# A graph message-passing kernel: order of the set-up, keys of two groups spread by TensorE, another order at the end, and 358 selections for 355

## The chip, the cores and the metric

The kernel runs on one core of a Trainium2 chip. The metric is the device time of one execution in microseconds (us), less is better. The engines are TensorE (PE, matrix products; its weight loads are shown as PEld), VectorE (DVE), ScalarE (ACT), GpSimd (POOL) and SyncE (SP). SP, ACT and POOL have queues from which DMAs are issued; each engine takes its instructions in the order of the program.

## The reference

```python
# N = 6250 nodes, E = 200000 edges sorted by dst, F = H = 64, M = 9, D = 32; AVG_DEG = 16
w    = silu(edge_attr_32 @ W1 + b1) @ W2 + b2                 # E x 9
msg  = einsum('ef,em,fmg->eg', x[src], edge_attr_9 * w, W_tp) # E x 64
agg  = segment_sum(msg, dst, N) / sqrt(AVG_DEG)
emb  = silu(node_vec[:, None] @ Wn1 + bn1) @ Wn2 + bn2
gamma, beta = split(emb, 2)
out  = layernorm(x + agg * (1 + gamma) + beta)
```

Everything is float32.

## The kernel before, in words

**Groups.** The edges lie in 1563 tiles of 128 (`NT`), taken in 98 groups (`NBLK`) of 16 tiles (`KB`), the last one of 11. Since edges are sorted by destination, the 128 edges of a tile reach only a window of 8 nodes (`W`), and a group reaches 128 window columns.

**Rows of x.** A tile needs the 128 rows x[src], one to a partition, in `hs[g]`. They come in three ways. Most tiles are gathered by an indirect DMA on POOL (L91), one instruction to a tile, 6 groups ahead (`AHEAD`), with 7 buffers. In every sixth group (`SPG`: 7, 13, ..., 97) the first tile comes by 128 DMAs of one row each from SP's queue (`load_rows`, L106). And the last 3 or 4 tiles of a group are *picked* on TensorE: x stands in SBUF as seven slices (`xs`), each number split in two parts whose sum it is; `pick(g, t)` multiplies a one-hot matrix (`hot_k`) with both parts of the seven slices, 14 matmuls into one PSUM tile `px` (L475), and DVE takes the wanted seventh of each result (`xm`, L484) and adds up (L486). `picked(g)` is the number of picked tiles of a group; in all there are 355 picked tiles, 1192 gathered ones and 16 that come by rows.

**Keys.** `hot_k` (DVE, L460) compares a key with a counter. The key of an edge must stand on all partitions, with edges along the free axis. Set-up computes the keys of all 392 picked columns with nine steps on DVE (L205 to L217), transposes them on TensorE in four pieces, stores them as float16 in DRAM (`kd`, L224), and `load_keys` reads those of two groups back, broadcast over the partitions (`kr`, L391). `keys(g)` copies a group's into PSUM on ACT (`pk`, L454).

**A group's other work.** `hidden(g)`: first layer on TensorE (L403) and silu on ACT (L411). `second(g)`: second layer (L420), bias on ACT (`p2s`, L423). `weights(g)`: two transposes (L430) and products on DVE that make `a`, 72 columns a tile (L442). `windows(g)`: for each tile one product of `hs` and `a` into `pz` (L504), which ACT copies to `zt` in four strided pieces for 8 tiles (L514). `project(q)`, for two groups: ten-fold product with W_tp (L543; L538 for the single last group), a transpose and the split in two parts `r`, and one-hot matrices `c` (L528). `place(q)`: puts the window columns to the nodes (`ps`, L559). `bring`: transposes back (L576) and calls `finish`, the gate, the residual and the layer norm for two blocks of 128 nodes (L670 to L683; the square root on ACT, L680), whose last line stores to `out`.

**Order.** There is no scheduler: all engines run the program's order. The loop over blocks `i` writes it out by hand: gather of group i+6; loads; rows by SP; `keys(i+2)`; `pick(i+1, 0)` with the node work of older groups among its matmuls; `hots`; `hidden(i+2)`; `second(i+1)`; `windows(i)`; `project` in odd blocks; `pick(i+1, 1)` with `weights(i+1)` and the transpose of `project` among its matmuls; the other picks of group i+1. The last two groups' `windows` come at the ends of their blocks.

**Set-up.** `setup` issues the loads, builds constants on POOL and DVE, gathers the first six groups, and splits x into `xs`: for each of seven slices ACT copies it, reordered, into PSUM (L292) and casts it to the first part (L293), and DVE subtracts for the second (L294). Among the slices stand the first keys and one-hot matrices, and `pick(0, 0)` follows the last slice. `base` spreads the first destination of each tile over the partitions with a product by ones (`p_b`, L242) and subtracts it from `dst` (`rel`, L243).

Of the kernel before, what the change touches and what calls it, by code (L numbers as in the profile page):

```python
# [7 lines left out]
F32 = mybir.dt.float32  # L8
# [41 lines left out]
def picked(g):  # L50

    return Q - (3 * g % 8 < 3)
# [7 lines left out]
def gnn_resnorm_kernel(ctx: ExitStack, tc: tile.TileContext, x, src, dst, dst_row, ea, sh, cn,  # L60
# [18 lines left out]
    with ExitStack() as fast:  # L79
# [54 lines left out]
        def setup(temp):  # L134
# [3 lines left out]
            nc.sync.dma_start(src_i[:, 0:AHEAD * KB], src[:, 0:AHEAD * KB])  # L138
            for q in range(4):
                nc.sync.dma_start(w1bd[q * D:(q + 1) * D, (q % 2) * H:(q % 2 + 1) * H], w1)  # L140
            nc.sync.dma_start(src_i[:, AHEAD * KB:], src[:, AHEAD * KB:])
            xb_r = xb.rearrange("p j f -> p (j f)")
            row_i = xb_r[0:1, 0:NBLK * KB].bitcast(I32)
            nc.scalar.dma_start(row_i, dst[0:1, :])
# [4 lines left out]
            for s in range(2):  # L149
                nc.scalar.dma_start(b1c[s * H:(s + 1) * H, :], b1.unsqueeze(1))  # L150

            xk = gam.rearrange("p (h l) f -> p h (l f)", h=J)
            x_v = x.rearrange("(p h l) f -> p h (l f)", h=J, l=J)
            for h0, h1 in ((0, 2), (2, 4), (4, 7)):
                nc.scalar.dma_start(xk[:, h0:h1, :], x_v[:, h0:h1, :])
            load(0)
            for s in range(2):
                nc.sync.dma_start(w2p[s * H:(s + 1) * H, s * M:(s + 1) * M], w2)
            nc.sync.dma_start(dst_i, dst)
# [18 lines left out]
            row_f = xb_r[0:1, NBLK * KB:2 * NBLK * KB]  # L178
            nc.scalar.copy(row_f, row_i)
            first_t = temp.tile([NBLK, KB], F32)  # L180
            nc.scalar.copy(first_t, first_i)
# [5 lines left out]
            nc.vector.tensor_add(ident2, ident[:, 0:F], ident[:, F:P])  # L187
            zero = temp.tile([P, 1], F32)
            nc.vector.memset(zero, 0.0)
            for k in range(2):  # L190
                nc.vector.memset(ht[k][H:H + 1], 1.0)
            nc.vector.memset(wtc2[F:P, 4], 0.0)
            ones1 = temp.tile([1, P], F32)
            nc.vector.memset(ones1, 1.0)
            nc.vector.memset(eps, EPS)
            nc.vector.tensor_copy(nk, nk_i)
            nc.vector.tensor_copy(wi, n_i[:, 0:W])
            nc.vector.tensor_copy(li, n_i[:, 0:J])


            zt_r = zt.rearrange("p a c k w -> p (a c k w)")
            s_f, kp, kh, rest, t0, t1 = [zt_r[:, k * C:(k + 1) * C] for k in range(6)]
            ti = [t.bitcast(I32) for t in (t0, t1)]
            s_f = s_f.rearrange("p (g k) -> p g k", k=Q)
            nc.vector.tensor_copy(s_f[:, 0:NBLK - 1, :],  # L205
                                  src_i.rearrange("p (g k) -> p g k", k=KB)[:, 0:NBLK - 1, KB - Q:])
            nc.vector.tensor_copy(s_f[:, NBLK - 1, :], src_i[:, NT - Q:NT])
            s_f = s_f.rearrange("p g k -> p (g k)")
            nc.vector.tensor_scalar(ti[0], s_f, 2675.0, None, op0=ALU.mult)
            nc.vector.tensor_scalar(ti[0], ti[0], 17, None, op0=ALU.logical_shift_right)  # L210
            nc.vector.tensor_copy(kp, ti[0])
            nc.vector.scalar_tensor_tensor(rest, kp, -float(J * J), s_f, op0=ALU.mult, op1=ALU.add)
            nc.vector.tensor_scalar(ti[1], rest, 37.0, None, op0=ALU.mult)
            nc.vector.tensor_scalar(ti[1], ti[1], 8, None, op0=ALU.logical_shift_right)
            nc.vector.tensor_scalar(kh, ti[1], float(P), None, op0=ALU.mult)
            kf = s_f
            nc.vector.tensor_add(kf, kp, kh)  # L217
            for c0 in range(0, C, P):
                n = min(P, C - c0)
                p_kt = psum.tile([P, P], F32, tag=("s", "r")[c0 // P % 2], name=f"p_kt{c0}")  # L220
                nc.tensor.transpose(p_kt[0:n], kf[:, c0:c0 + n], ident)
                kt = t1[:, c0 // 2:c0 // 2 + P // 2].bitcast(F16)
                nc.scalar.copy(kt[0:n], p_kt[0:n])
                nc.sync.dma_start(kd[c0:c0 + n, :], kt[0:n])  # L224
            nc.vector.scalar_tensor_tensor(jl, kh, -float(J) / P, rest, op0=ALU.mult, op1=ALU.add)
            hidden(0, act=False)
            load_keys(0)
            load_keys(LB)
            for c in range(KB // 4):
                for s in range(2):  # L230
                    q = c * D + s * M
                    nc.sync.dma_start(b2c[q:q + M, :], b2.unsqueeze(1))


            rel_v = rel.rearrange("p (a b c) -> p a b c", a=2, b=2)
            dst_v = dst_i.rearrange("p (a b c) -> p a b c", a=2, b=2)
            row_v = row_f.rearrange("p (a b c) -> p a b c", a=2, b=2)

            def base(a_):
                p_b = psum.tile([P, 2, KB * P // 4], F32, tag="p1", name=f"p_b{a_}")  # L240
                for b_ in range(2):
                    nc.tensor.matmul(p_b[:, b_, 0:NBLK * KB // 4], ones1, row_v[:, a_, b_, :], start=True, stop=True)  # L242
                nc.vector.tensor_sub(rel_v[:, a_], dst_v[:, a_], p_b[:, :, 0:NBLK * KB // 4])  # L243


# [8 lines left out]
            nc.vector.tensor_copy(pw, pw_i)  # L254

            def ids():
                p_nid = psum.tile([P, NBLK], F32, tag="s", name="p_nid")
                nc.tensor.matmul(p_nid, sel, first_f, start=True, stop=True)
                nc.vector.scalar_tensor_tensor(nid, p_nid, pw, lo, op0=ALU.add, op1=ALU.subtract)

            def between(h):

                if h == 0:
                    p_f = psum.tile([KB, NBLK], F32, tag="s", name="p_f")
                    nc.tensor.matmul(p_f, first_t, ident[0:NBLK, 0:NBLK], start=True, stop=True)
                    nc.scalar.copy(first_f, p_f)
                elif h == 1:
                    keys(0)
                    hots(0, 0, Q)
                elif h == 3:  # L270
                    p_cn = psum.tile([P, NJ], F32, tag="s", name="p_cn")
                    nc.tensor.matmul(p_cn, cn_j, ident[0:NJ, 0:NJ], start=True, stop=True)
                    cn_s = temp.tile([P, NJ], F32)
                    nc.scalar.copy(cn_s, p_cn)
                    nc.sync.dma_start(cn_d, cn_s)
                    nc.sync.dma_start(wn1c, wn1.rearrange("o h -> h o"))
                    nc.sync.dma_start(bn1c, bn1.unsqueeze(1))
                    gate_load(0)
# [10 lines left out]
            for h in range(J):  # L289
# [5 lines left out]
                if h == 1:  # L295
                    hidden_act(0)
# [13 lines left out]
            for f in weights(0):  # L310
                f()
# [547 lines left out]
```

## Time and profile before

| | us |
|---|---|
| timed runs: median of 3 (lowest, highest) | 2508.16 (2504.98, 2527.9) |
| profiled execution, own time | 1521.78 |
| profiled execution, span from first to last instruction | 1519.9 |
| PE busy | 1438.0 |
| POOL busy | 1129.3 |
| DVE busy | 1135.4 |
| ACT busy | 526.1 |

The mean granted TensorE clock of the profiled execution is 0.983. Its own time is 986 us under the median of the timed runs. The profile is one execution; busy time is the time in which an engine has an instruction in work, the idle time before an instruction is put down to what released it, and "issue" stands where the profile shows nothing that was waited for. Lines written L91 are those of the kernel before.

### The profile page before, as it was taken

To read this page: it belongs to the slowest core of one execution; us is meant where nothing else is said; L and a number is where in the kernel's file an instruction comes from. 1 tells how busy PE (TensorE), PEld (TensorE's weight loads), DVE (VectorE), ACT (ScalarE), POOL (GpSimd) and SP (SyncE) were. 2 spreads that over 40 slices of the span, in tenths; PEclk is the share of its full clock that TensorE was granted. 3 is DMA by queue.
4 is the path that set the end of the run, shared out by engine and by line. 5 is a ranking of instruction groups with operands and counts; after the bars stand their busy time and mean duration, and the time that the engine had idled before them with its cause. 6 is when DMAs were issued, how large, how long until landed. Compare 5 with 4: busy or idle time off the path is not lost.

```text
span 1519.9 us, 34363 instructions
## 1 busy us (share of the span) xinstructions
PE 1438.0 (95%) x10810; PEld 1192.7 (78%) x10810; DVE 1135.4 (75%) x1987; ACT 526.1 (35%) x1335; POOL 1129.3 (74%) x1201
## 2 busy tenths in 40 slices
PE   4998999999999999999999999989998998999995
PEld 2787888888888788888888888878777887878784
DVE  5686777877877878777777877768677777687773
ACT  4223342433423333332423424424233333333331
POOL 7777777777777777777777777777777777777772
PEclk9999999999999999999999999999999999999997
DMA  6422232222222222222322222222222222222210
GB/s 171 95 56 63 54 76 53 64 59 70 65 56 72 58 63 71 60 63 54 74 59 55 72 52 63 71 54 61 53 72 53 59 55 71 52 55 59 73 29 15
DMA packets 90939, 96.16 MB, mean 63 GB/s; under 512 B 37161, under 2 KB 51451, under 8 KB 90748
## 3 DMA queue, kind: packets, MB, share of 16 engines
q0 software_dynamic: 38144, 39.14, 13.4%
q1 hardware_dynamic: 51842, 53.09, 12.1%
q8 instruction: 88, 1.44, 0.4%
q10 hardware_dynamic: 762, 1.64, 0.3%
q14 instruction: 103, 0.84, 0.2%
HBM read 92.04 MB, written 1.73 MB: 62 GB/s over the span
## 4 chain that ended last, share of the span: by engine, by line
PE 57%; POOL 18%; issue 9%; SPq 5%; DMA 5%; DVE 4%; ACT 2%; DVEq 0%; POOLq 0%; ACTq 0%
PE px L475 41%; POOL hs L91 18%; PE pz L504 5%; DMA hs<-in_x_dram,src_i 4%; PE p L403 3%; SPq L106 3%; PE pt L543 3%; PE p L420 2%; SPq L101 2%; PE p L430 1%; PE ps L559 1%; PE ps L589 0%; ACT st L411 0%; DVE hot_k L460 0%; DVE xm L484 0%
## 5 line engine op out<-in xcount | busy, mean ns | idle before, releaser
L91 POOL DMA_INDIRECT hs<-in_x_dram,src_i x1192 | 1128.0, 946 | 364.3 <-issue 330.7
L475 PE MATMUL px<-xs,hot_k 128*128 128x448 f32 x4970 | 1090.6, 372 | 9.4 <-DVE xs L294 8.8
L475 PEld LDWEIGHTS px<-xs,hot_k 128*128 128x128 f32 x4970 | 896.8, 189 | 93.9 <-issue 10.9
L484 DVE SCALAR_TENSOR_TENSOR xm<-li,jl,px 128x448 f32<-128x448 f32 x355 | 240.3, 677 | 203.6 <-PE px L475 202.0
L460 DVE TENSOR_TENSOR hot_k<-pk,nk 128x896 fp32r<-128x896 f32 x355 | 370.6, 1082 | 3.1 <-ACT pk L454 3.1
L411 ACT ACTIVATE st<-p,b1c 128x1024 f32<-128x1024 f32 x98 | 109.5, 1118 | 405.4 <-PE p L403 405.1
L486 DVE TENSOR_REDUCE hs<-xm 128x64 f32<-128x448 f32 x355 | 220.1, 620 | 12.2
L514 ACT COPY zt<-pz 64x160 f32<-64x160 f32 (+2 forms) x784 | 213.5, 272 | 40.6 <-PE pz L504 28.0
L504 PEld LDWEIGHTS pz<-a,hs 128*64 128x64 f32 x3126 | 110.2, 142 | 68.1 <-issue 61.2
L504 PE MATMUL pz<-a,hs 128*64 128x72 f32 x3126 | 124.6, 234 | 27.0 <-DMA hs<-in_x_dram,src_i 11.5
L442 DVE TENSOR_TENSOR a<-oh,p 128x1152 f32<-128x1152 f32 x98 | 132.7, 1354 | 3.3
L436 DVE TENSOR_TENSOR p<-p,sh 128x72 f32<-128x72 f32 x196 | 47.0, 240 | 100.9 <-ACT rt L546 45.2
L403 PE MATMUL p<-ea,w1bd 64*128 64x512 f32 x392 | 113.3, 655 | 0.0
L565 ACT COPY carry<-ps 128x128 f32<-128x128 f32 x48 | 12.8, 266 | 273.4 <-PE ps L559 273.4
L420 PEld LDWEIGHTS p<-st,w2p 128*32 128x32 f32 x784 | 15.8, 108 | 83.2 <-issue 39.0
L420 PE MATMUL p<-st,w2p 128*32 128x256 f32 x784 | 63.5, 396 | 7.8 <-DVE xb L356 7.8
L680 ACT ACTIVATE var<-var,eps 128x2 f32<-128x2 f32 (+1 forms) x25 | 7.4, 295 | 179.2 <-DVE var L679 179.2
L543 PE MATMUL pt<-zt,wtc 128*64 128x128 f32 x960 | 64.3, 281 | 2.6 <-ACT zt L514 1.7
L543 PEld LDWEIGHTS pt<-zt,wtc 128*64 128x64 f32 x960 | 55.0, 142 | 3.8 <-ACT zt L514 1.9
L454 ACT CAST pk<-kr 128x384 f32<-128x384 f16 (+1 forms) x98 | 53.8, 549 | 2.2 <-DMA kr<-kd 2.2
L430 PE MATMUL p<-ident,p2s 128*128 128x128 f32 x196 | 53.3, 273 | 0.0
L403 PEld LDWEIGHTS p<-ea,w1bd 64*128 64x128 f32 x392 | 30.0, 187 | 28.7 <-issue 28.0
(122 smaller groups left out, 529.0 us busy)
## 6 DMA issues: line engine op xcount, KB each, us to landing
hs<-in_x_dram SPq DMA_DIRECT2D x2048, 0.2 KB
ea<-in_ea_dram SPq DMA_DIRECT2D x49, 512.0 KB
hs<-in_x_dram,src_i POOLq DMA_INDIRECT x1192
kr<-kd SPq DMA_DIRECT2D x49, 256.0 KB
sh<-in_sh_dram SPq DMA_DIRECT2D x49, 144.0 KB
cb<-cn_d SPq DMA_DIRECT2D x12, 128.0 KB
out_dram<-o SPq DMA_DIRECT2D x24, 64.0 KB
gam<-in_x_dram ACTq DMA_DIRECT2D x2, 448.0 KB
```

The costliest lines, as they stand in the source:

```text
L91: hs_dma[g] = [nc.gpsimd.indirect_dma_start(out=hs[g][:, t - g * KB, :], out_offset=None, in_=x, in_offset=bass.IndirectOffsetOnAxis(ap=sr ...
L403: nc.tensor.matmul(p1[:, i, :], w1bd[i * 64:(i + 1) * 64, :], e[i * 64:(i + 1) * 64, :], start=True, stop=True)
L411: nc.scalar.activation(st[g], p1_t.pop(g), AF.Silu, bias=b1c)
L420: nc.tensor.matmul(p2[g][c * D:(c + 1) * D, 0, :].rearrange("p (i e) -> p i e", i=2), w2p, s[:, :, c * P:(c + 1) * P], start=True, stop=True)
L442: nc.vector.tensor_mul(a[g], oh_t.pop(g)[:, :, None, :].to_broadcast([P, KB, M, W]), sw.unsqueeze(3).to_broadcast([P, KB, M, W]))
L460: nc.vector.tensor_tensor(hot_k[g, t], pk_t[g][:, t, None, :].to_broadcast([P, J, P]), nk.unsqueeze(2).to_broadcast([P, J, P]), op=ALU.is_ ...
L475: nc.tensor.matmul(px.rearrange("p f l -> p (f l)"), hot_k[g, t][:, h, :], xs[i][:, h].rearrange("p f l -> p (f l)"), start=(h == 0 and i ...
L484: nc.vector.scalar_tensor_tensor(xm, li[:, None, :].to_broadcast([P, F, J]), jl[:, c:c + 1], px, op0=ALU.is_equal, op1=ALU.mult)
L486: nc.vector.tensor_reduce(hs[g][:, tiles(g) - q + t, :], xm, AX.X, ALU.add)
L504: mm = nc.tensor.matmul(pz[v * F:(v + 1) * F, k // 2].rearrange("p m w -> p (m w)"), hsg[:, k0 + k, :], ag[:, k0 + k].rearrange("p m w -> ...
L514: nc.scalar.copy(z[h * F:(h + 1) * F, 0:5 - h, k0 + v:k0 + n:2, :].rearrange("p m k w -> p k m w"), pz[v * F:(v + 1) * F, 0:(n + 1 - v) // ...
L543: nc.tensor.matmul(pt[h * F:(h + 1) * F, 0, 0:P], wtc2[:, c, :], z[h][:, c], start=(c == 0), stop=(c == 4))
```

## The change

It has five parts.

1. **Set-up order.** The pieces of x go to the head of ACT's queue, in four DMAs for three. On SP's queue come the first sources, the first weights, the edge features of group 0 apart from those of group 1 (`load(0, split=True)`), and the first 32 columns of `dst` with their first destinations broadcast by DMA (`row_i`, for the product by ones of `base`). All else is loaded after group 0's work in the program.
2. **Splitting x.** The copy of each slice into PSUM is dropped; DVE subtracts from SBUF.
3. **Keys of groups 0 and 1.** `keys_of(0, LB)` works out 8 columns only; `keys_first` scales the identity by a key column on DVE and multiplies by a matrix of ones on TensorE, so that the key of edge e stands in column e on all partitions. The other 384 columns take the old way (`keys_rest`), after group 0's picks.
4. **The end.** `windows(96)` moves to its usual place. The picks of group 97 have `project(48)` and `place(48)` among them. `windows(97)` takes its second half of tiles, the picked ones, first, writes to two PSUM tiles, and half of its copies are DVE's. Stores of results are issued by SP at the start of the next block, in a list `stores`.
5. **358 picks.** Three picked tiles are 34 groups' (every third, and the last) in place of 37 groups'; three gathers fewer.

```diff
 def picked(g):
-    return Q - (3 * g % 8 < 3)
+    return Q - (g % 3 == 0 or g == NBLK - 1)
@@ setup
             nc.sync.dma_start(src_i[:, 0:AHEAD * KB], src[:, 0:AHEAD * KB])
+            xk = gam.rearrange("p (h l) f -> p h (l f)", h=J)
+            x_v = x.rearrange("(p h l) f -> p h (l f)", h=J, l=J)
+            for h0, h1 in ((0, 1), (1, 2), (2, 4), (4, 7)):
+                nc.scalar.dma_start(xk[:, h0:h1, :], x_v[:, h0:h1, :])
             for q in range(4):
                 nc.sync.dma_start(w1bd[q * D:(q + 1) * D, (q % 2) * H:(q % 2 + 1) * H], w1)
+            for s in range(2):
+                nc.scalar.dma_start(b1c[s * H:(s + 1) * H, :], b1.unsqueeze(1))
+            row_i = xb.rearrange("p j f -> p (j f)")[:, 0:NBLK * KB].bitcast(I32)
+            load(0, split=True)
+            nc.sync.dma_start(dst_i[:, 0:2 * KB], dst[:, 0:2 * KB])
+            nc.sync.dma_start(row_i[:, 0:2 * KB], rows(dst[0, 0:2 * KB], P))
             nc.sync.dma_start(src_i[:, AHEAD * KB:], src[:, AHEAD * KB:])
...
+            def keys_first(g, kf, tag):
+                pk_t[g] = psum.tile([P, Q, P], F32, tag=tag, name=f"pk{g}")
+                for t in range(picked(g)):
+                    c = (g + 1) * Q - picked(g) + t
+                    d0 = NBLK * KB + c * P
+                    dg = xb.rearrange("p j f -> p (j f)")[:, d0:d0 + P]
+                    nc.vector.tensor_scalar(dg, ident, kf[:, c:c + 1], None, op0=ALU.mult)
+                    nc.tensor.matmul(pk_t[g][:, t, :], ones, dg, start=True, stop=True)
+            def keys_rest(kf):
+                for c0 in range(LB * Q, C, P):
+                    n = min(P, C - c0)
+                    p_kt = psum.tile([P, P], F32, tag="r", name=f"p_kt{c0}")
+                    nc.tensor.transpose(p_kt[0:n], kf[:, c0 - LB * Q:c0 - LB * Q + n], ident)
+                    kt = zt_r[:, 6 * C + c0 // 2:6 * C + c0 // 2 + P // 2].bitcast(F16)
+                    nc.scalar.copy(kt[0:n], p_kt[0:n])
+                    nc.sync.dma_start(kd[c0:c0 + n, :], kt[0:n])
+            def split(h):
+                xh = gam[:, h * J:(h + 1) * J, :].rearrange("p l f -> p f l")
+                nc.scalar.copy(xs[0][:, h], xh)
+                nc.vector.tensor_sub(xs[1][:, h], xh, xs[0][:, h].bitcast(F32))
+            kf = keys_of(0, LB)
+            keys_first(0, kf, "r")
+            hots(0, 0, 1)
+            for h in range(J):
+                split(h)
+            pick(0, 0)
+            hots(0, 1, Q)
+            keys_first(1, kf, "s")
+            hots(1, 0, 1)
+            nc.vector.tensor_copy(wi, n_i[:, 0:W])
+            nc.vector.tensor_sub(rel[:, 0:2 * KB], dst_i[:, 0:2 * KB], row_i[:, 0:2 * KB])
+            near(0)
+            pick(0, 1)
+            hots(1, 1, Q)
+            hidden(0)
+            second(0)
+            pick(0, 2, [[lambda: None, lambda: None], weights(0)])
+            hidden(1)
+            nc.sync.dma_start(dst_i[:, 2 * KB:], dst[:, 2 * KB:])
+            nc.sync.dma_start(row_i[:, 2 * KB:], rows(dst[0, 2 * KB:], P))
+            load(LB)
+            keys_rest(keys_of(LB, NBLK))
+            load_keys(LB)
...
-                xp = psum.tile([P, F, J], F32, tag="px" if h in (2, 3) else "pz", name=f"x{h}", bufs=2)
-                nc.scalar.copy(xp, xh)
-                nc.scalar.copy(xs[0][:, h], xh)
-                nc.vector.tensor_sub(xs[1][:, h], xp, xs[0][:, h].bitcast(F32))
...
@@ windows
-            for k0 in range(0, nk, ZT):
+            end = g == NBLK - 1
+            for k0 in reversed(range(0, nk, ZT)) if end else range(0, nk, ZT):
...
-                        nc.scalar.copy(
+                        (nc.vector.tensor_copy if end and v else nc.scalar.copy)(
@@ blocks
+                while stores:
+                    stores.pop(0)()
...
-                if i < NBLK - 2:
+                if i < NBLK - 1:
                     windows(i)
-                turn = project(i // 2) if i % 2 == 1 else []
+                turn = project(i // 2) if i % 2 == 1 and i < NBLK - 1 else []
...
+                if i == NBLK - 2:
+                    sums(i + 1)
+                    turn = project(i // 2)
+                    ps = psum.tile([P, 2 * P], F32, tag="s", name="ps_l")
+                    pick(i + 1, 2, [turn])
+                    more = place(i // 2, ps)
+                    if picked(i + 1) < Q:
+                        for f in more:
+                            f()
+                        more = []
+                    pick(i + 1, 3, [more])
+                    continue
...
+            for f in bring(NJ - 3, NJ - 1, psum.tile([P, FB, F], F32, tag="s", name="py_l")):
+                f()
+            windows(NBLK - 1)
             project(NBLK // 2)
```

## The prediction

> **What bounds the kernel now.** First the page's busy shares, then the costliest groups, then the stretches of the span, the waits, and the timelines of start and end.
>
> ```profile
> PE 1438.0 (95%) x10810; PEld 1192.7 (78%) x10810; DVE 1135.4 (75%) x1987; ACT 526.1 (35%) x1335; POOL 1129.3 (74%) x1201
> L91 POOL DMA_INDIRECT hs<-in_x_dram,src_i x1192 | 1128.0, 946 | 364.3 <-issue 330.7
> L475 PE MATMUL px<-xs,hot_k 128*128 128x448 f32 x4970 | 1090.6, 372 | 9.4 <-DVE xs L294 8.8
> ```
>
> By busy time TensorE (PE) is the bound and POOL has a quarter to spare. That is the wrong reading: nearly all of POOL's idle time stands before gathers and is put down to "issue", nothing that it waits for. The timeline of POOL gives the real pace:
>
> ```profile
> 2.92 1.11 POOL L91 DMA_INDIRECT hs<-in_x_dram,src_i  x1 [0.97 <-DMA src_i<-in_src_dram]
> ...
> 1493.22 0.94 POOL L91 DMA_INDIRECT hs<-in_x_dram,src_i  x1 [0.30 <-issue]
> ```
>
> From the first start to the last are 1191 intervals in 1490.3 us: 1.2513 us each, with no stop between. POOL gathers from 2.9 us to 1494.2 us of a span of 1519.9. The stretches say where PE meets it:
>
> ```profile
> 600.00:800.00 200.00, 197.56 (x1533) 164.58 (x1532) 156.40 (x279) 71.62 (x185) 151.45 (x160) 1.00 0.27 63
> 1000.00:1200.00 200.00, 188.89 (x1394) 157.99 (x1389) 143.39 (x236) 64.43 (x168) 151.21 (x160) 0.98 0.26 62
> ```
>
> PE (first busy figure) is full until about 980 us and then loses 11 us in 200; POOL (fifth) is the same in both. In the waits of PE, its idle time before windows (L504) is a wait for gathered rows:
>
> ```profile
> PE pz L504 <- DMA hs<-in_x_dram,src_i: 11.5, 8, 4.4
> PE pz L504 <- issue: 10.8, 6, 4.8
> PE pz L504 <- DMA out_dram<-o: 2.5, 1, 2.5
> ```
>
> I read all three as that, since they begin where the last gather of the group ended only 2 to 3 us before: 24.8 us that PE has in hand. So the order is: group 0's windows at 55.75 us stand 36 us behind their gathers (the thirteenth gather, counted off on POOL, ended at 19.4), PE takes 14.7 us a group and POOL 15.2, the lead of POOL is eaten by about group 62, and from there POOL sets the pace. The last of it is in the timeline of PE:
>
> ```profile
> 1472.36 1.22 PE L504 MATMUL pz<-a,hs 128*64 128x72 f32 x32 [0.41 <-DMA hs<-in_x_dram,src_i]
> ...
> 1485.71 8.08 PE L475 MATMUL px<-xs,hot_k 128*128 128x448 f32 x38
> 1493.72 1.22 PE L504 MATMUL pz<-a,hs 128*64 128x72 f32 x32
> ...
> 1502.01 1.67 PE L504 MATMUL pz<-a,hs 128*64 128x72 f32 x22
> 1506.35 2.40 PE L538 MATMUL pt<-wtc,zt 128*128 128x64 f32 x10 [2.67 <-ACT zt L514]
> ```
>
> **What the Trainium skill says.** "Perfetto Trace Analysis", section GPSIMD Engine Instruction, calls a GpSimd span unreliable and asks for start-to-start spacing; the trace agrees: 1.2513 us against a printed 0.946. The same page, section DMA Instruction — SWDGE (GPSIMD), says that the end shown is that of the last descriptor and not of the data; here windows 95 begin at 1472.36, 1.9 us after the last gather of their group ended at 1470.5. "FP8 and Floating Point Precision", section TensorE Precision Notes, gives true FP32 four passes; no row here has a 128x128 FP32 product by a ones matrix, so I use the row of the key transposes below.
>
> **The change part by part.**
>
> *358 picks for 355.* Three gathers fewer: 3 x 1.2513 = 3.75 us off POOL. On PE three picks more: 28 pick matmuls took 6.74 us in the chain of waits (0.241 each), so 3 x 14 x 0.241 = 10.1 us, and on DVE 3 x (1.08 + 0.68 + 0.62) = 7.1 us, which 25% of idle time hides. The 10.1 us fall into the 24.8 us in hand. Without that cover they would count in full.
>
> *The start.* Before, ACT makes two strided copies per slice of x:
>
> ```profile
> 21.94 0.92 ACT L292 COPY x<-gam 128x448 f32<-128x448 f32 x1
> 22.79 0.95 ACT L293 CAST xs<-gam 128x448 fp32r<-128x448 f32 x1
> ```
>
> and the first group's keys go through DRAM, as the chain of waits shows:
>
> ```profile
> 13.18 4.61 DMA kd<-zt
> 18.19 3.73 DMA kr<-kd
> ```
>
> The L292 copies go, 7 x 0.92 = 6.4 us, and so does the key trip of groups 0 and 1 (13.18 to 21.92, then a key copy). In its place come seven scaled identities (DVE, as ident took 0.29: 2.0 us) and seven products (the four passes of the key transposes took 1.52 us, some 0.4 each: 2.7 us). That is the unseen operation: from 0 if it lies wholly beside the landing of x to 4.7 us if nothing hides it, and not below 0, because the trip that it spares is counted apart; I take 2, since keys of two groups (9 DVE steps on 8 columns, some 0.15 each as the smallest casts) can be ready by 5 us. With x moved to the head of ACT's queue (four DMAs there, issue about 0.65 each) I place it by 8 us; seven copies of 0.95 end at 14.7 and pick 0 by 16 us, against 31.98. So PE's first pick comes 16 us earlier. But 384 of the 392 key columns are now worked out behind group 0. DVE's nine steps, 4.3 us, fall about 33 to 38 us; transposes and cast 1; then the kd landing (4.61), the kr landing (about 4.1 with issue): keys of group 2 at about 48 us. `keys(2)` is an early ACT instruction of block 0; behind it on ACT stand the hidden layer of group 2, p2s of group 1 and the z copies of group 0, and PE needs p2s in the middle of pick (1,1). On SP the two w2p and eight b2c loads (1.19 and 3.75 us of issue) move ahead of the kd stores and are out by about 11 us, long before group 0's p2s at 27; the rest of dst_i, its broadcast row and load(2) follow without a wait. Then SP stands at the kd stores till 38, and w_tp, the gate's weights, src_r and the reload of xb stand behind them and behind the kr load; w_tp is wanted first, by project 0 at some 64 us, and is issued by 50. So I give back 9 of the 16: windows 1 at about 63 us instead of 70.2. Since POOL starts at the same 2.9 us (src_i is still SP's first; x on the other queue may cost it 0 to 0.5 us), this adds 7 us to PE's reserve, 24.8 + 7 - 10.1 + (-3.75) = 18 us, and nothing to the end.
>
> *The end.* In order: the last gather ends at 1494.16 - 3.75 = 1490.4. Behind group 95 there are now 13 + 7 gathers where there were 13 + 6, so windows 95 may begin at 1472.4 - 3.75 - 1.25 = 1467.4. Windows 96 now come before pick (97,1); seven gathers follow its group: 1490.4 - 8.8 + 1.9 = 1483.5, and PE, there at 1479.5, waits 4. Then: windows 1.15, pick (97,1) with weights 3.6, project 48 1.3, pick (97,2) with its turn 3.5 = 1493.0; xm and reduce 1.3, the yt sum 0.3, bring 0.5 = 1495.1. The finish of nodes 46 and 47 then starts at 1495.15 where it started at 1502.00: 6.85 us earlier. It stands ahead of the last z copies on ACT and DVE, as it does now on ACT: from its first step to its o took 2.96 us, and 1.35 more until zt was full. With half of these copies on DVE I take 0.9, so 0.45 us is saved. The rest of the chain (10 projection matmuls 2.4, r and c 0.8, place 0.56, bring 0.7, finish 2.5, store and landing 6.0) stays. Sum: 6.85 + 0.45 = 7.3 us. The fourth pick of group 97 is gone; without it pick (97,3) would add 3.4. The gathers of group 97 land by 1492.3, before PE asks, so they don't bind.
>
> *Stores one block later.* SP stood 45.2 + 14.2 us waiting for o and its neighbours (waits of SP, L684). That goes, worth nothing while SP's row loads keep ahead: those of group 97 ended at 1484.0, windows 97 began at 1502.0. The split of load(0), psum tags and the moved small steps cost nothing beside the above: all have later users.
>
> **Sum.** The profiled execution took 1521.78 us for its span of 1519.9; minus 7.3 gives 1514.5. The median of the timed runs is 2508.16, 986 us longer, and no view shows where that lies. I assume that it stays as it is and that the saving is the same: 2508.2 - 7.3 = 2500.9. If each step were stretched in proportion (2508/1522 = 1.65) it would be 12: 2496. One per cent, 25 us, is about what a measurement of this kernel can tell from no change, so both are no change.
>
> **The rivals.**
>
> 1. *Another engine than POOL sets the timed runs, and what I call hidden counts.* If SP's queue is slow there (22 row loads already take it 12.7 us of 15), its 59.4 us of waits for stores count, perhaps two thirds, 40 us; with the end 7: about 2460. If it is PE and the start counts in full: 16 + 8 - 10 = 14, 2494. For: the unexplained 986 us. Against: in the trace neither binds at the end. Over 1% faster: 0.19.
>
> 2. *PE sets the timed runs, and it has no reserve.* Place: the pick matmuls and block 0. Price: 10.1 x 1.65 = 17 us for three picks, and if the key trip stalls ACT until 65 us instead of 48 the start comes 17 us late; less the end's 7: +27, 2535. It decides once PE's work is over POOL's by more than the 18 us left in hand. For: PE is 95% busy. Against: PE waits for POOL in the last third. Over 1% slower: 0.16.
>
> 3. *The change does nothing it says:* the start is hidden and the end loses to the finish of 46 and 47 what it gains: 2508. It falls within 1%.
>
> **How the numbers follow.** Forecast (2501) 0.55, rival 3 and small misses 0.10: within 1% 0.65. Range: the end can give 3 to 12 us, the timed runs before lie within 23 us of each other, and half of each outer rival is to be inside: 2468 to 2533.
>
> **What would show it.** POOL's gathers should still be 1.25 us apart, 1189 of them, the last starting at about 1489.5. Pick 0 should end near 16 us, windows 1 come near 63, PE's waits at L504 amount to 15 to 25 us, and the last o come 6 to 8 us sooner. Wrong would be: gaps on POOL, no PE waits for gathers after 1000 us, or a finish of nodes 46 and 47 that starts after 1500.

## The result and the profile after

The changed kernel took 2524.21 us (median of 22 runs, 2507.8 to 2545.96), the kernel before 2515.32 us (22 runs, 2491.08 to 2551.16): ratio 1.009, 95% interval [1.006, 1.0119]. It is 0.9% slower, where 7 us less (0.3%) had been forecast. The time lies in the predicted range; the sign is wrong. Ratios, here and below, are formed from the faster runs of each kernel alone, so they differ by up to half a per cent from the quotient of the medians beside them.

The profile of before that the prediction was worked from ran at 1522 us, a pace at which none of these timed runs ran, while the profile after (span 2521.4 us, own time 2523.18) ran at theirs; so this document sets the profile after beside a later trace of the kernel before (label before_look2, span 2529.3 us, own time 2531.16) and calls the two paces the 1520 us pace and the 2520 us pace.

First the page of the kernel after, busy shares and costliest groups (busy, mean ns of one | idle time before them, and what ended most of it):

```profile
PE 1667.1 (66%) x10857; PEld 1356.4 (54%) x10857; DVE 1155.0 (46%) x2017; ACT 519.6 (21%) x1320; POOL 1128.2 (45%) x1198
...
L91 POOL DMA_INDIRECT hs<-in_x_dram,src_i x1189 | 1126.9, 948 | 1284.7 <-PE pz L506 947.9
L473 PE MATMUL px<-xs,hot_k 128*128 128x448 f32 x5012 | 1270.6, 408 | 539.4 <-DVE xm L482 472.1
...
L482 DVE SCALAR_TENSOR_TENSOR xm<-li,jl,px 128x448 f32<-128x448 f32 x358 | 242.4, 677 | 792.9 <-remote 567.5
```

Set these against the lines of the prediction. POOL's gathers take what they took (948 ns for 946), but they no longer run without a stop: POOL stands 947.9 us waiting until windows (L506) have freed a buffer. PE is busy two thirds of the time and waits 472.1 us for `xm`, which frees `px`; DVE in turn stands 567.5 us before `xm` for "remote", that is, for something that no record of this core explains. No engine is near full. The chain that ended last says the same:

```profile
PE 38%; another core or an unknown queue 32%; DVE 15%; issue 10%; ACT 4%; DMA 0%; DVEq 0%; ACTq 0%
```

There is one core here, so the 32% is no other core. The timeline of the same kernel, hidden(0) and hidden(1), shows what stands behind it (start, duration, engine, line; in brackets the idle time before):

```profile
29.16 1.13 PE L401 MATMUL p<-ea,w1bd 64*128 64x512 f32 x4
...
43.93 1.11 ACT L409 ACTIVATE st<-p,b1c 128x1024 f32<-128x1024 f32 x1 [25.75 <-remote]
...
68.80 1.13 PE L401 MATMUL p<-ea,w1bd 64*128 64x512 f32 x4
...
121.63 1.11 ACT L409 ACTIVATE st<-p,b1c 128x1024 f32<-128x1024 f32 x1 [56.23 <-remote]
```

By the records the four products of hidden(1) were done at 69.93 us; ACT, which stood idle for them, got them at 121.6, 52 us later. The Trainium skill, "Perfetto Trace Analysis", section Tensor Engine Instruction (MATMUL, LD_WEIGHTS), says that such an end is computed from the instruction's size and not observed. This trace agrees: the work was later than its record, so the 66% too is partly modelled. This wait ends while POOL stands still: a gather starts every 1.25 us up to 113.37, then none before ACT goes on. The wait for hidden(0) ended among the gathers, 13.6 us after the record (43.93 for 30.29), so results do come there, but late. Windows by stretch (PE, PEld, DVE, ACT, POOL busy, clock, DMA share, GB/s) show the end of the kernel:

```profile
2200.00:2400.00 200.00, 143.84 (x907) 116.66 (x905) 91.88 (x151) 41.02 (x106) 92.73 (x98) 0.83 0.16 38
2400.00:2480.00 80.00, 75.78 (x560) 62.78 (x560) 60.50 (x104) 27.50 (x68) 6.63 (x7) 0.98 0.10 26
```

Per 100 us PE makes 454 matmuls in the first stretch, a mean over bursts of gathers (98 of them, some 120 us) and the rests between them, and 700 in the second, where POOL has all but finished; the work is the same. At the 2520 us pace a block is thus a burst of gathers (some 15 us), in which TensorE's results come late, and a rest in which PE catches up: 25.2 us from one windows to the next (groups 8 to 88), where the prediction had 15.2.

It is not TensorE alone that is late. SP's row loads (`load_rows`) contain register instructions that name no tile. Their count and their shortest, median and longest time in ns, in the prediction's trace of the kernel before, in the kernel after and in pool_plain (a kernel below, whose DMAs on POOL are not indirect):

```profile
L106 SPq FUSED_REGOPS  x2048: 37/37/51, 52.8 to 1483.9; - x187
L106 SPq FUSED_REGOPS  x2048: 2/37/1397, 147.2 to 2491.9; - x187
L105 SPq FUSED_REGOPS  x2048: 37/37/51, 68.0 to 1467.4; - x187
```

The median is the same, but at the 2520 us pace some take over a microsecond, and 22 row loads take 12.9, 21.2 and 14.3 us (from 1396.8 us on) where the prediction had 12.7. VectorE's `xm` takes 677 ns in all of these kernels. So beside the gathers at least two engines, TensorE and SP, get on more slowly; what holds them up is not shown.

The kernel before at this pace has the same picture, so it is not the change's doing:

```profile
L91 POOL DMA_INDIRECT hs<-in_x_dram,src_i x1192 | 1128.1, 946 | 1284.9 <-PE pz L504 930.5
L475 PE MATMUL px<-xs,hot_k 128*128 128x448 f32 x4970 | 1265.2, 409 | 573.3 <-DVE xm L484 528.6
L484 DVE SCALAR_TENSOR_TENSOR xm<-li,jl,px 128x448 f32<-128x448 f32 x355 | 240.4, 677 | 887.5 <-remote 647.0
```

### The profile page after: what moved, and what is told of

Its sections match the earlier page's. It is cut to its first block, busy times and chain, and to the rows that moved or that the text cites. A ratio compares the mean times of both kernels' runs of the same rounds, so it can differ in the third digit from the quotient of the medians.

```text
span 2521.4 us, 34479 instructions
## 1 busy us (share of the span) xinstructions
PE 1667.1 (66%) x10857; PEld 1356.4 (54%) x10857; DVE 1155.0 (46%) x2017; ACT 519.6 (21%) x1320; POOL 1128.2 (45%) x1198
## 3 DMA queue, kind: packets, MB, share of 16 engines
q0 software_dynamic: 38048, 39.04, 8.1%
q8 instruction: 89, 1.46, 0.2%
## 4 chain that ended last, share of the span: by engine, by line
PE 38%; another core or an unknown queue 32%; DVE 15%; issue 10%; ACT 4%; DMA 0%; DVEq 0%; ACTq 0%
PE px L473 26%; DVE xm L482 4%; PE pz L506 4%; PE p L401 3%; PE pt L546 2%; DVE hs L484 2%; DVE hot_k L458 2%; DVE a L440 2%; PE p L418 2%; DVE c L530 1%; ACT zt L516 1%; ACT st L409 1%; DVE p L434 1%; PE p L428 1%
## 5 line engine op out<-in xcount | busy, mean ns | idle before, releaser
L91 POOL DMA_INDIRECT hs<-in_x_dram,src_i x1189 | 1126.9, 948 | 1284.7 <-PE pz L506 947.9
L473 PE MATMUL px<-xs,hot_k 128*128 128x448 f32 x5012 | 1270.6, 408 | 539.4 <-DVE xm L482 472.1
L473 PEld LDWEIGHTS px<-xs,hot_k 128*128 128x128 f32 x5012 | 1007.9, 212 | 672.6 <-DVE xm L482 496.9
L482 DVE SCALAR_TENSOR_TENSOR xm<-li,jl,px 128x448 f32<-128x448 f32 x358 | 242.4, 677 | 792.9 <-remote 567.5
L516 ACT COPY zt<-pz 64x160 f32<-64x160 f32 (+1 forms) x780 | 212.6, 273 | 15.6 <-PE pz L506 6.8
L418 PE MATMUL p<-st,w2p 128*32 128x256 f32 x784 | 72.8, 435 | 163.4 <-DVE xb L350 90.1
L506 PEld LDWEIGHTS pz<-a,hs 128*64 128x64 f32 x3116 | 128.1, 157 | 77.2 <-issue 73.4
L506 PE MATMUL pz<-a,hs 128*64 128x72 f32 x3116 | 147.2, 252 | 27.0 <-issue 26.5
L527 DVE TENSOR_TENSOR r<-pt,r 128x128 fp32r<-128x128 f32 x48 | 14.0, 291 | 193.6 <-issue 98.8
L526 ACT CAST r<-pt 128x128 fp32r<-128x128 f32 x48 | 12.8, 266 | 362.2 <-remote 301.4
L546 PE MATMUL pt<-zt,wtc 128*64 128x128 f32 x960 | 79.9, 326 | 9.2 <-ACT st L409 9.2
L546 PEld LDWEIGHTS pt<-zt,wtc 128*64 128x64 f32 x960 | 69.4, 171 | 11.1 <-ACT st L409 10.7
```

Of the source, the lines that this page charges most:

```text
L91: hs_dma[g] = [nc.gpsimd.indirect_dma_start(out=hs[g][:, t - g * KB, :], out_offset=None, in_=x, in_offset=bass.IndirectOffsetOnAxis(ap=sr ...
L418: nc.tensor.matmul(p2[g][c * D:(c + 1) * D, 0, :].rearrange("p (i e) -> p i e", i=2), w2p, s[:, :, c * P:(c + 1) * P], start=True, stop=True)
L473: nc.tensor.matmul(px.rearrange("p f l -> p (f l)"), hot_k[g, t][:, h, :], xs[i][:, h].rearrange("p f l -> p (f l)"), start=(h == 0 and i ...
L482: nc.vector.scalar_tensor_tensor(xm, li[:, None, :].to_broadcast([P, F, J]), jl[:, c:c + 1], px, op0=ALU.is_equal, op1=ALU.mult)
L506: mm = nc.tensor.matmul(pz[v][v * F:(v + 1) * F, k // 2].rearrange("p m w -> p (m w)"), hsg[:, k0 + k, :], ag[:, k0 + k].rearrange("p m w ...
L516: (nc.vector.tensor_copy if end and v else nc.scalar.copy)(z[h * F:(h + 1) * F, 0:5 - h, k0 + v:k0 + n:2, :].rearrange("p m k w -> p k m w ...
```

## Experiments

The kernels of one table ran on the same chip and share the runs of the kernel before; between tables the chip changes, so only ratios go from one to the next, and with care. The pace went with the chip: all runs of the first table took 1513 to 1527 us, all runs with indirect gathers in the four others 2442 to 2558 us. What sets the first chip apart is not known.

### The parts alone

Edits: `picks_only` is the kernel before with the new `picked(g)`; `setup_only` has the new set-up alone (parts 1 to 3); `end_only` the new end and the later stores (part 4); `before_look` is the kernel before.

> The kernel before, once more, for its trace at the pace of the timed runs (some 2510 us). Both theories take it that here too a result of TensorE reaches DVE and ACT late while POOL gathers. Theory START (the changed set-up does its work inside the first unbroken run of gathers, where TensorE's results come late): the windows of group 0 start before 125 us here, against 138.7 us in the changed kernel. Theory PICKS (at this pace gathers and TensorE's work add up, so that a pick costs more than a gather saves): the windows of group 0 start within 8 us of 138.7, and the middle is as long as in the changed kernel less some 8 us.

> The kernel before with the 358 picks alone. Theory PICKS: three picks at 3.4 us or more on TensorE against three gathers at 1.25 us: slower by 6 to 9 us, ratio 1.0025 to 1.004. Theory START: the picks cost nothing or gain, ratio 0.997 to 1.001. If the pattern of the groups matters instead of the number, the ratio may reach 1.006.

> The kernel before with the new set-up alone (old picks, old end). Theory START: slower by 12 to 25 us, ratio 1.005 to 1.010, and the windows of group 0 start 15 us or more later than in the kernel before. Theory PICKS: ratio 0.998 to 1.002.

> The kernel before with the new end and the stores issued one block later (old picks, old set-up). Both theories: faster by 5 to 12 us, ratio 0.995 to 0.998, since the last groups run after POOL has ended and nothing delays them there; if SP's waits for stores counted, more: 0.99.

All of these ran at the 1520 us pace (before: 1521.17 us, 26 runs), so what these texts expect of the other pace could not be tested. In its place they test the prediction's own model, at the pace that it was made from:

| kernel | us | ratio to before |
|---|---|---|
| before_look (one run) | 1521.5 | |
| picks_only | 1513.88 | 0.9952 [0.9938, 0.9965] |
| setup_only | 1525.56 | 1.0032 [1.002, 1.0044] |
| end_only | 1522.71 | 1.0013 [1.0006, 1.0019] |

The picks alone give 7.3 us. That the forecast for all five parts was also 7.3 is chance, since the other parts, measured alone, gain nothing here. The timeline of picks_only has the last gather and the last windows:

```profile
1488.59 0.94 POOL L91 DMA_INDIRECT hs<-in_x_dram,src_i  x1 [0.30 <-issue]
...
1494.09 1.67 PE L504 MATMUL pz<-a,hs 128*64 128x72 f32 x22 [0.16 <-PE py_l L576]
```

The last gather starts 4.6 us earlier than in the prediction's lines, windows 97 at 1494.1 for 1502.0: the three gathers (3.75 us) and the fourth pick of group 97 (put at 3.4). The 42 added pick matmuls cost nothing: at this pace the reserve of PE is real. The set-up alone loses 4.4 us; its timelines of POOL, ACT and PE:

```profile
3.69 1.11 POOL L91 DMA_INDIRECT hs<-in_x_dram,src_i  x1 [1.74 <-DMA src_i<-in_src_dram]
...
17.65 1.45 POOL L91 DMA_INDIRECT hs<-in_x_dram,src_i  x1 [0.30 <-issue]
...
9.76 1.28 ACT L181 ACT_TABLE_LOAD   x1 [9.76 <-DMA b1c<-in_b_dram]
...
72.33 1.22 PE L499 MATMUL pz<-a,hs 128*64 128x72 f32 x32
```

The sources land 0.77 us later (3.69 for 2.92) and single gathers take up to 2.08 us (1.46 in the first 20 us) while the loads of set-up land; POOL ends 2.2 us later, and POOL sets the end here. The profiled execution, the fastest of six, is 2.3 us longer than before_look, which POOL's delay accounts for; the rest of the 4.4 us between the medians is not traced. ACT comes to its first instruction only at 9.76, pick 0 ends at 18.9 for 16, the key copy of group 2 comes at 51.3 for 48, and windows 1 at 72.3 for the predicted 63 (70.2 before): the early start is given back before group 1. The end alone gains nothing where POOL sets it, and is 1.5 us slower: windows 96 wait 3.94 us for the last gathers, and with the fourth pick left in group 97, windows 97 start at 1502.2 as before.

### The parts at the 2520 us pace

Edits: `old_picks` is the changed kernel with the old `picked(g)`; `end_picks` the changed kernel with the old set-up; `after_look` and `before_look2` are the two kernels.

> The changed kernel beside the kernel before. If the kernel before takes some 1521 us here: the parts measured alone add up (picks -7.3, set-up +4.4, end +1.5 us, and the end gains 4 more where group 97 has three picks), 1514 to 1519 us, ratio 0.996 to 0.9985. If it takes some 2515 us: 2524 us again, ratio 1.006 to 1.012.

> The kernel before, for its trace. At 2515 us: theory START says that windows of group 0 start before 125 us (138.7 in the changed kernel); theory PICKS says within 8 us of 138.7. At 1521 us: as in its trace shown before.

> The changed kernel with the 355 picks of the kernel before: new set-up and new end. At 1521 us: ratio 1.002 to 1.006. At 2515 us: theory START, that the set-up is what costs there, 1.004 to 1.012; theory PICKS 0.996 to 1.001.

> The changed kernel with the set-up of the kernel before: 358 picks and new end. At 1521 us: ratio 0.993 to 0.996, faster than the changed kernel by 3 to 6 us. At 2515 us: theory START 0.995 to 1.0; theory PICKS 1.004 to 1.009.

| kernel | us | ratio to before (2524.42, 43 runs) |
|---|---|---|
| after_look | 2534.81 | 1.0048 [1.0023, 1.0073] |
| old_picks | 2517.32 | 0.9946 [0.9919, 0.9972] |
| end_picks | 2556.01 | 1.012 [1.0088, 1.0151] |

Only one edit lies between the first two: the picks cost 1.0048 - 0.9946 = 1.0%, some 26 us (17.5 by the medians). Set-up and end together gain 0.5%; with the new picks the set-up is worth 0.7%. So theory START falls and the loss is the picks', and it is partly paid back. The traces agree: windows 0 begin at 138.51 us in before_look2 and at 138.71 in after, as PICKS had it, and not before 125; the ratios of old_picks and end_picks lie on PICKS' side, a little beyond its ranges. How much of it is the end can be read from the timelines; before_look2 (first three lines, windows 95, windows 97, projection 48) and after (last two, windows 95 and projection 48):

```profile
2481.31 1.22 PE L504 MATMUL pz<-a,hs 128*64 128x72 f32 x32
...
2511.28 1.67 PE L504 MATMUL pz<-a,hs 128*64 128x72 f32 x22
...
2515.62 2.40 PE L538 MATMUL pt<-wtc,zt 128*128 128x64 f32 x10 [2.67 <-ACT zt L514]
```

```profile
2479.99 1.22 PE L506 MATMUL pz<-a,hs 128*64 128x72 f32 x32
...
2507.74 2.36 PE L540 MATMUL pr<-wtc,zt 128*128 128x64 f32 x10 [3.35 <-DVE zt L516]
```

From windows 95 to the end of the span it is 48.0 us before and 41.4 after: 6.6 us gained, against the 7.3 of the prediction. In old_picks, where group 97 keeps its fourth pick, the same stretch takes 42.7 us, so that pick is worth 1.3 us there (put at 3.4). Since gathers are long done there, this part runs at full speed at both paces.

### Number of picks, and the gathers themselves

`spread358` has 358 picks in the pattern of before, `two_picks` two picks in every group:

```diff
-    return Q - (g % 3 == 0 or g == NBLK - 1)
+    return Q - (3 * g % 8 < 3 and g not in (24, 48, 72))   # spread358
+    return 2                                               # two_picks: 196 picks, 1351 gathers
```

`no_pool` loads the rows of a group by one plain DMA from ACT's queue; `pool_plain` keeps POOL's 1189 DMAs but takes the indices away:

```diff
-            hs_dma[g] = [nc.gpsimd.indirect_dma_start(
-                out=hs[g][:, t - g * KB, :], out_offset=None, in_=x,
-                in_offset=bass.IndirectOffsetOnAxis(ap=src_i[:, t:t + 1], axis=0))
+            hs_dma[g] = [nc.gpsimd.dma_start(hs[g][:, t - g * KB, :], x_rows[:, t % NJ, :])
                 for t in range(g * KB + (g in SPG), g * KB + tiles(g) - picked(g))]
```

> The changed kernel with its 358 picks spread otherwise: the pattern of the kernel before, and a fourth pick in groups 24, 48 and 72. If the kernel before takes some 2520 us here: theory NUMBER (each pick more and gather less costs some 8 us) says 1.005 to 1.009 of the kernel before, as the changed kernel; theory PATTERN (every third group with three picks is what costs) says 0.994 to 0.998, as the changed kernel with 355 picks. At some 1521 us, where POOL sets the end: 0.997 to 1.000 under both.

> The changed kernel with two picks in every group: 196 picks, 1351 gathers. At 2520 us: theory OVERLAP (TensorE goes at about a third of its speed while POOL gathers, so that a group costs its TensorE work and two thirds of its gather time) says 5.6 us of TensorE work a group less and 2.1 us of gathers more, 21 us a group: about 2100 us, ratio 0.84. Theory FIXED (the 986 us are a cost that the picks have no part in): POOL's 159 gathers more at 1.25 us add 200 us, ratio 1.08. At 1521 us: POOL's end, 1351 x 1.2525 + 30 = 1722 us, ratio 1.13, under both.

> The changed kernel in which the rows of the gathered tiles are not gathered: one plain DMA a group from ACT's queue loads as many rows of x, in their order, so other rows than those wanted; POOL has nothing to do after set-up. At 2520 us: theory OVERLAP says TensorE's own pace, 1460 to 1520 us; theory FIXED 2400 us or more. At 1521 us: 1460 to 1500 us, TensorE being the bound.

> The changed kernel in which POOL issues the same 1189 DMAs of 128 rows as plain ones, without an index (other rows than those wanted). If it is POOL's writing of descriptors that slows TensorE, the time stays near that of the changed kernel at 2520 us; if it is the lookup by index, it falls to about 1500 us. At 1521 us: 1500 to 1520 us if POOL takes as long for a plain DMA, else less.

| kernel | us | ratio to before (2528.94, 43 runs) |
|---|---|---|
| spread358 | 2521.38 | 0.9965 [0.9937, 0.9994] |
| two_picks | 2536.51 | 1.0028 [1.0008, 1.0048] |
| no_pool (one run) | 1665.08 | |
| pool_plain (one run) | 1498.71 | |

The number is acquitted: 358 picks in the old pattern are not slower, as theory PATTERN had it. two_picks moved by 0.3% only, which neither theory expected (0.84 or 1.08), but it does not show that picks are free, for another queue holds it. Its waits of PE and two lines of its timeline of SP:

```profile
PE p L401 <- DMA ea<-in_ea_dram: 185.2, 39, 17.1
...
1395.44 22.93 SPq L106 DMA_DIRECT2D hs<-in_x_dram  x22
...
1421.20 22.75 SPq L106 DMA_DIRECT2D hs<-in_x_dram  x22
```

The row loads of one group take SP some 23 us of a block of 25.4, SP waits for others 126.7 us in the whole kernel (478.8 in the changed one), and the edge features, which SP loads too, come late: PE waits 185.2 us for them, where the changed kernel has no such wait. What a pick costs at this pace is left open by it.

That the gathers set the pace is shown by pool_plain. Its page:

```profile
PE 1438.2 (96%) x10857; PEld 1195.8 (80%) x10857; DVE 1147.0 (77%) x2017; ACT 515.5 (34%) x1320; POOL 630.1 (42%) x1198
...
q0 software_dynamic: 38048, 39.04, 8.6%
...
L91 POOL DMA_DIRECT2D hs<-in_x_dram x1189 | 628.9, 537 | 756.5 <-PE pz L505 725.1
L481 DVE SCALAR_TENSOR_TENSOR xm<-li,jl,px 128x448 f32<-128x448 f32 x358 | 242.4, 677 | 204.1 <-PE px L472 202.3
```

As many DMAs from the same queue, with the same 38048 packets and 39.04 MB, run beside a PE that is 96% full; no wait is put down to "remote" before `xm`, and the kernel takes 1499 us on the chip where the kernel before took 2529. It is a single execution, as is no_pool, but none of the 85 other runs of this table took under 2498 us. So neither that POOL issues DMAs nor their packets and bytes are the brake, but something that goes with their being indirect: the look-up of 128 indices each, POOL's longer work on each (948 ns for 537), or the scattered rows (the plain ones read neighbouring rows); these are not told apart. The lower granted clock (0.813 in the profile after, 0.985 here) looks too small a cause: PE's busy time by the records is 229 us longer (1667.1 for 1438.2), the kernel 1025 us. And within the profile after the clock is 0.50 where PE has one matmul on record (80 to 120 us) and 0.98 where PE is full (2400 to 2480 us). no_pool agrees, less cleanly: without POOL it takes 1665 us (1460 to 1520 expected), and its PE waits 107.1 us for edge features (L400), which are late there for another reason.

The Trainium skill, "SBUF — State Buffer", section "SBUF: two separate sides", says that a DMA cannot be slowed by a compute operation "and vice versa", and that PE, ACT and DVE's own ports wait on no one. pool_plain agrees; the gathered kernels show TensorE and SP held up beside POOL's indirect DMAs (454 matmuls in 100 us for 700; register instructions of up to 1397 ns for 51), by which way is not shown.

### Place of the lighter groups

`phase1` and `blocks12` have 358 picks too; `setup_again` is the new set-up with old picks and end.

```diff
-    return Q - (g % 3 == 0 or g == NBLK - 1)
+    return Q - (g % 3 == 1 or g == 0)      # phase1
+    return Q - (g % 12 < 4)                # blocks12
```

> The changed kernel with its 358 picks in another phase of the same period: three picks in groups 1, 4, 7, ... and in group 0. Theory PERIOD (what costs is that groups i+1 and i+7 always have the same number of picks, since 3 divides 6, the lead of the gathers; so much TensorE work meets few gathers and little meets many) says, at some 2525 us for the kernel before, 1.003 to 1.010, as in the changed kernel. Theory PLACE (it is where the three-pick groups fall among loads, projections and the last group) says 0.993 to 1.000. At 1521 us: 0.996 to 1.0 under both.

> The changed kernel with 358 picks of period 12: three picks in groups 0 to 3 of every 12, so that a group with three picks always has one with four picks six groups later. Theory PERIOD says 0.985 to 0.9965, no slower than the spread pattern; if any regular pattern costs, 1.003 or more. At 1521 us: 0.996 to 1.0.

> The kernel before with the new set-up alone, at the pace of the timed runs. By difference of the kernels run so far (changed kernel 1.0048, without the new set-up 1.012) it gains: 0.990 to 0.996 at 2525 us, with the windows of group 1 ten us or more earlier than the 164.0 us of the kernel before. At 1521 us: 1.003 again.

| kernel | us | ratio to before (2526.85, 34 runs) |
|---|---|---|
| phase1 | 2497.47 | 0.9831 [0.9775, 0.9886] |
| blocks12 | 2510.55 | 0.9929 [0.9896, 0.9961] |
| setup_again | 2519.02 | 0.9971 [0.9943, 0.9998] |

The same period at another phase has the lowest ratio of all, 1.7% faster than before, with a wide spread: its six runs go from 2474.74 to 2524.56 us, and by the medians it is 1.2%. blocks12 lies where theory PERIOD had it, but phase1 does not (1.003 to 1.010 expected), so the period of three alone is not what costs; where the three-pick groups stand counts. The set-up alone gains 0.3% here, just short of what was expected, and with old_picks that leaves some 0.25% for the end, 6 us, as in the timelines.

Why the phase counts was then tried. In the groups of `SPG`, which get one tile by rows, the changed kernel has four picks and so 11 gathers, next to groups with 13; phase1 has three picks there and at most 12 in all odd groups. `rows6` and `phase1_rows6` move SPG, `phase2` is the third phase:

```diff
-SPG = range(7, NBLK, 6)
+SPG = range(6, NBLK, 6)                              # rows6, phase1_rows6
-    return Q - (g % 3 == 0 or g == NBLK - 1)
+    return Q - (g % 3 == 1 or g == 0)                # phase1_rows6
+    return Q - (g % 3 == 2 or g in (0, 97))          # phase2
```

> The changed kernel with the groups that get one tile by rows moved by one: SPG = 6, 12, ..., 96 in place of 7, 13, ..., 97. The picks stay the changed kernel's (three in every third group from 0, and in 97). The gathers of six groups in a row become 12, 12, 12, 13, 12, 12 in place of 13, 11, 12, 13, 12, 12. Theory EVEN (what made the other phase 2.5% faster is that no group has 11 gathers and the next 12 or 13: the bursts of POOL are even): ratio to the kernel before 0.98 to 0.99. Theory PHASE (it is the place of the lighter picks against the blocks' other work, odd or even and every sixth, that counts; the gathers' evenness does not): 1.00 to 1.01, as the changed kernel.

> The faster phase of the picks (three in groups 1, 4, 7, ... and in 0) with the groups of rows moved by one to 6, 12, ..., 96: the gathers of six groups become 11, 13, 12, 12, 13, 12 in place of 12, 12, 12, 12, 13, 12; picks and their number are unchanged. EVEN: the gain is gone, 1.00 to 1.01. PHASE: the gain stays, 0.98 to 0.99.

> The third phase: three picks in groups 2, 5, 8, ..., and in 0 and 97, 358 picks in all; groups of rows as in the changed kernel (7, 13, ...). The gathers of six groups are 12, 11, 13, 12, 12, 13 from a multiple of six on. EVEN: as the changed kernel, 1.00 to 1.01. PHASE says nothing of this phase that is fixed beforehand: the three-pick groups fall on even and odd places in turn as in the other two, so anything from 0.98 to 1.01; a value near 0.985 speaks against EVEN.

| kernel | gathers of six groups, from 12 on | us | ratio to before (2471.42, 23 runs) |
|---|---|---|---|
| rows6 | 12, 12, 12, 13, 12, 12 | 2501.64 | 1.0107 [1.004, 1.0173] |
| phase1_rows6 | 11, 13, 12, 12, 13, 12 | 2512.09 | 1.0134 [1.0072, 1.0195] |
| phase2 | 12, 11, 13, 12, 12, 13 | 2465.22 | 1.0001 [0.9974, 1.0028] |

Neither theory's numbers come out: EVEN had 0.98 to 0.99 for rows6, PHASE the same for phase1_rows6. But the step from 0.9831 to 1.0134 does not show that moving the rows destroys the gain of the phase, for the two ran on different chips, and most of the step is the kernel before, which is 2.2% faster on this one (2471.42 for 2526.85 us); phase1_rows6 itself is 0.6% slower than phase1 (2512.09 for 2497.47). Neither phase1 nor the changed kernel ran on this chip, and rows6 and phase1_rows6 have four runs each. What holds on one chip is that phase2 is 1.1% and 1.3% below the other two by the ratios, with as many picks, so the places of the lighter groups or of the rows count. Why they count stays unexplained. Of these patterns of period three phase1 is the only one in which every odd group, whose block also carries a projection, has 12 gathers; that was noticed afterwards and not tested.

## Why the prediction was wrong, point by point

- **The step that failed:** "986 us longer, and no view shows where that lies. I assume that it stays as it is". The 986 us are not a part beside the kernel to which a saving is added; they lie inside every block (25.2 us for 15.2): beside POOL's indirect gathers TensorE and SP get on more slowly, and POOL stands 947.9 us for buffers instead of setting the end. pool_plain shows their size: 1499 us for the same instruction counts. A saving worked out at the one pace does not carry over to the other: the same new picks gave -7.3 us at the 1520 us pace and some +26 us at the 2520 us pace.
- **"The 10.1 us fall into the 24.8 us in hand."** Right at the 1520 us pace (picks_only -7.3 us, nothing paid for 42 matmuls). At the pace of the timed runs the new pattern costs 1.0%, some 26 us (old_picks and after_look). The term that was put at nothing is the largest of the sum. It is not the added matmuls that cost: spread358 has as many and is not slower. In which way the pattern costs is open.
- **Gathers 1.25 us each, 1189 of them:** held at both paces within a burst. That POOL runs unbroken and sets the end held at the 1520 us pace alone; POOL stood 947.9 us for buffers in the profile after. This was the sign that the prediction named for being wrong ("gaps on POOL").
- **The start.** "Nothing to the end" and "windows 1 at about 63" were both off. At the 1520 us pace the set-up costs 4.4 us (slower first gathers; windows 1 at 72.3). At the 2520 us pace windows 1 come at 153.1 after and 164.0 before, and the set-up gains 0.3% (0.7% with the new picks). That an earlier start counts there because POOL sets no bound is likely and not shown.
- **The end:** size nearly right, 6.6 us for 7.3 in the traces, though at the 2520 us pace the gathers, which were to give 3.75 of it, ended long before. At the 1520 us pace the end alone loses 1.5 us with the heavier group 97; the whole change was not run there, so the sum of 7.3 was never put to the test at its own pace.
- **Stores one block later.** "That goes" is wrong: SP still waits for results at the stores, 62.2 us in end_only (59.4 before) and at the 2520 us pace 198.3 us (152.8 before). At the 1520 us pace it was worth nothing, as said.
- **Rival 1** (SP's queue slow in the timed runs) has a point that the forecast lacked: the row loads are stretched there. But its saving did not come, since the waits at the stores stayed.
- **Rival 2** (PE without a reserve, 2535) is nearest: the picks count and the sum is a loss. But its start, 17 us late, came early instead, and its price was per pick, where spread358 shows none for three picks more in the old pattern.

The sum of the parts at the timed pace: picks +26 us by the ratios, set-up -7 to -18 (alone, or with the new picks), end -6; that gives +2 to +13 us, and the two comparisons of the whole gave 1.0048 and 1.009, +12 to +23. The two ranges barely meet. What is settled is which part loses; why that pattern loses is open. That the time fell inside the predicted range is luck: the mechanism behind the forecast did not hold.

## What to carry to other kernels

When the profiled execution and the timed runs differ by 1.65, the bound read from the profile may be that of another regime, as here: get a trace at the timed pace before costing anything, and do not carry the difference along as a constant. Where an unknown queue holds a third of the chain and consumers wait long after a matmul's recorded end, look at which engine is active in those stretches, and take its kind of work away rather than its amount. In such a regime a cheap change of phase (three-pick groups moved by one) was worth more, 1.2 to 1.7% on the one chip where it ran, than the worked-out savings; phase1, blocks12, old_picks and spread358 were all faster than the kernel before on their chips, where the changed kernel was slower in both of its comparisons.

## What the hardware did that was not expected

- At the 2520 us pace, beside bursts of indirect gathers, TensorE's results came up to 52 us after their recorded ends, and PE made 454 matmuls in 100 us, bursts and rests together, for 700 without gathers; at the 1520 us pace the same gathers, at the same 1.25 us spacing, did no such thing.
- In the same kernels register instructions of SP took up to 1397 ns (median 37), where they take at most 51 at the 1520 us pace and in pool_plain.
- A plain DMA of 128 rows occupied POOL for 537 ns against 948 for an indirect one, with equal packets and bytes.
- With 196 picks in place of 358, and 162 more gathers, the time moved by 0.3%; there SP's queue had hardly a wait left.
